# Four edits to the planner's priorities and prices in a Mamba scan kernel: transposes that go ahead of late jobs, gates of six tiles per SiLU, a cheaper GpSimd product, a stricter yield to decays

## The chip, the cores and the metric

The kernel runs on one core of a Trainium2 chip. The core has five engines with an instruction queue each: TensorE (PE in the profile, its weight loads PEld), VectorE (DVE), ScalarE (ACT), GpSimd (POOL) and SyncE (SP), which issues the DMAs. Each queue is worked off in order; semaphores hold an instruction until its inputs are there. The metric is the device time in microseconds. The profile is of one execution.

## The reference

Two residual layers on x of shape (2, 48, 48, 768). Layer 0 is neighbourhood attention (7 x 7 window, 12 heads). Layer 1 is a Mamba block that scans the 2304 tokens of each image forwards and backwards, with 1536 inner channels and 16 states per channel. All is float32.

```python
x = x + _L0_conv_ref(_gn(x), w_qkv, w_out)              # attention
xz = einsum('bld,ed->bel', _gn(x) as tokens, in_proj_w)  # layer 1
out_f = _branch(xz, ...)
out_b = _branch(xz[:, :, ::-1], ..._b)[:, :, ::-1]
x = x + einsum('bdl,cd->blc', out_f + out_b, out_proj_w)

def _branch(xz, ...):
    x, z = (xz[:, :d_in], xz[:, d_in:])
    x = silu(_dwconv(x, conv_w, conv_b))                 # 4 taps
    dt, Bm, Cm = split(einsum('bdl,ed->bel', x, x_proj_w))
    delta = softplus(einsum('brl,dr->bdl', dt, dt_proj_w) + dt_proj_b)
    A = -exp(A_log)
    # per token: h = exp(delta*A)*h + (delta*x)*B ;  y = sum over 16 states of h*C
    y = _selective_scan(x, delta, A, Bm, Cm) + x * Dp
    return y * silu(z)
```

## The kernel before, in words

**Tiles and passes.** Channels lie on the 128 partitions: 12 channel tiles (ND). Tokens are cut into 6 chunks of 384 (CL). A pass is one chunk in one direction of one image; there are 24 passes of 12 tiles, 288 units. Image 0 goes forwards through its chunks, then backwards, then image 1.

**A unit (`scan`, L1179 on)** has four groups of four states. For each group: the B product (L1224) writes delta*x*B into a buffer hb, on DVE or POOL, as the planner chooses for three groups of the four (the first of them, g = 0, is DVE's alone); four decays exp(delta*A) (L1246, ACT) go two by two into the PSUM buffers da, of which there are two; two scans (L1257, DVE), each over two states, work in place in hb; the C product (L1272, POOL) multiplies hb by C; twelve transposes on PE (L1289, `add_up`) add the four states into py, transposed, after three transposes of x*Dp (L1305, `direct`) that open py. Then ACT copies py to yt (L1315). In a forward pass yt goes to memory. In a backward pass PE turns the sum of both directions back (`sums`, L1342), and DVE multiplies by the gate silu(z) (L1352). There are seven hb, one py and one du (a copy of delta*x in PSUM that DVE's B products read).

**Jobs beside the scans.** The in-projection of a chunk (`in_proj`) makes u (x after its four taps and SiLU, both directions) and the gates z, tile by tile: PE products (L382, mm_xin and mm_z), first taps on ACT (L928), three more per direction on DVE (L935), z copied by ACT (L955). After every KB = 3 tiles, `finish` runs one SiLU over a uz buffer (two of them) and stores it: a table load, the SiLU, a table load back (L961, L962). A u buffer holds three tiles in two directions, 2304 elements a partition; a z buffer holds three tiles, 1152. Softplus of the deltas (L1161, L1162) has two table loads as well. Then there are the x_proj products (mm_xd), the attention of image 1 (image 0's runs before the first scan) and the out-projections.

**What sets the order.** Nothing is issued as it is written. `Order.add` records each piece of work with its engine, an estimated time in ns, a key (in units: when it is wanted) and the buffers that it reads and writes. `Order.run` then plans: on each engine it looks at the ready works and picks the one with the lowest rank, the pair (start, but no less than 150 ns after the engine comes free; key - early). So among works that can start at once, the key decides, and a job with an old key goes ahead of the scan's own work. Works marked due are the decays, so this has effect on ACT alone: a work with a later key than the oldest unfinished scan work is put back by half of what it would delay the soonest decay beyond DUE ns. Where PE would idle long, filler transposes are put in (L1489). The program is issued in the planned order, so the estimates set the order only; the chip sets the times.

**Gate chunks.** Image 0's chunk 0 makes its gates late, by an `in_proj` without conv that has keys 41 to 47, and so do chunks 0 to 3 of image 1.

Of the kernel before, what the change touches and what calls it, by code (L numbers as in the profile page):

```python
# [16 lines left out]
P = 128  # L17
# [22 lines left out]
CL = 384  # L40
# [3 lines left out]
SG = 4  # L44
# [49 lines left out]
class Order:  # L94
# [3 lines left out]

    SEM = 90.0
    LOOK = 2.5  # L100
    DUE = 300.0
    GAP = 800.0
    TAIL = {"PE": 120.0, "ACT": 50.0, "DVE": 45.0, "POOL": 10.0, "SP": 0.0}

# [141 lines left out]
def tile_kernel(  # L246
# [72 lines left out]
    def sb(tag, shape, n, parts=1):  # L319
        return Buf(f"{tag}_{n}", wk, shape, tag, BUFS.get(tag, 1), parts)  # L320
# [8 lines left out]
    def add(eng, ns, fn, key, r=(), w=(), job=False, size=0, after=None, early=0, alt=None, due=False, opens=None):  # L329

        news = [x[0] if isinstance(x, tuple) else x for x in w]

        def issue():
            for v in news:
                if v.ap is None:
                    v.ap = v.pool.tile(v.shape, F32, tag=v.tag, name=v.name, bufs=v.bufs)
            fn()

        if eng == "PE":

            ns *= 1.04 if key < 0 else 1.05
        return order.add(eng, ns, issue, key, r, w, job, size, after, early, alt, due, opens)
# [4 lines left out]
    def act(n, pointers=0):  # L347
        return 60 + 90 * pointers + n * 0.833

    def dve(n):  # L350
        return 55 + n * 1.042
# [528 lines left out]
    def in_proj(b, i, start, end, conv=True, gate=True, nk=KB, tags=("uz",), banks=("mm",), proj=None):  # L880
# [67 lines left out]
        def z_tile(k, kk, nk, uz, s, key):  # L948
            m = f"{b}_{i}_{k}"
            part = (uz, s * nk + kk)  # L950
            (wz,) = weights(w_inT, [(0, DI + k * P)], f"z{m}", key, after=got)
            pz = ps("mm", f"z_{m}")
            product(pz, cl, [(wz, c, 0) for c in range(NC)], [(xc, c, HALO) for c in range(NC)], key, to=part)
            add(
                "ACT", act(cl), lambda: nc.scalar.copy(uz[:, s, kk, :cl], pz[:, :cl]), key + 0.05,  # L955
                r=[pz], w=[part], job=True,
            )

        def finish(k0, nk, uz, dsts, key):
            def silu():  # L960
                nc.scalar.activation(uz[:, :, :, :cl], uz[:, :, :, :cl], AF.Silu)  # L961
                nc.scalar.preload_act_table_set("natural_log_exp_and_others")  # L962

            add("ACT", 2600 + act(len(dsts) * nk * cl), silu, key, r=[uz], w=[uz], job=True)
            for s, dst in enumerate(dsts):
                add(
                    "SP", 400,
                    lambda s=s, dst=dst: nc.sync.dma_start(
                        rows_of(dst, k0, nk, l0, cl), uz[:, s, :, :cl]
                    ),  # L970
                    key + 0.1, r=[(uz, range(s * nk, (s + 1) * nk))],
                    w=[(dst, cols(l0, cl, k0, nk))], job=True, size=nk * P * cl * 4,
                )
# [3 lines left out]
        for x, k0 in enumerate(range(0, ND, nk)):  # L977
            if conv:
                uz = sb(tags[x % len(tags)], [P, 2, nk, CL], f"u{b}_{i}_{k0}", 2 * nk)
                for kk in range(nk):  # L980
                    k = k0 + kk
                    u_tile(k, kk, nk, uz, start + k * step, banks[k % len(banks)])
                finish(k0, nk, uz, dsts[:2], start + (k0 + nk) * step)
                if proj:
                    proj(uz, k0, nk, start + (k0 + nk) * step + 0.05)
            if gate:
                uz = sb(tags[x % len(tags)], [P, 1, nk, CL], f"z{b}_{i}_{k0}", nk)
                for kk in range(nk):
                    z_tile(k0 + kk, kk, nk, uz, 0, start + (k0 + kk) * step)
                finish(k0, nk, uz, dsts[-1:], start + (k0 + nk) * step)  # L990

    def staged(src, l0, cl, n, key, w=None, wsrc=None):

# [185 lines left out]
    def scan(ch, k, x, dlj, duj, vt):  # L1179
# [30 lines left out]
        def group(g):  # L1210
            m = f"{n}_{g}"
            now = at + 0.25 * g
            hb = sb("hb", [P, SG * W], m, SG + 1)
            body = (hb, range(SG))
            kept = lambda o: state[:, k, 2 * SG * g + o : 2 * SG * (g + 1) + o].rearrange(
                "p (j e) -> p j e", e=2
            )
            was = zero if ch["first"] else kept(0) if back else kept(1)

            def first():
                by, on = (dus[:, ju, :], nc.gpsimd) if filled.eng == "POOL" else (du[:, :W], nc.vector)
                on.tensor_mul(  # L1224
                    cells(hb, SG), by.unsqueeze(1).to_broadcast([P, SG, W]), bc[g].ap
                )

            if k == 0 or not ch["first"]:
                add(
                    "ACT", 98, lambda: nc.scalar.copy(bc[g][:, :, ends], was), now - 0.4,  # L1230
                    [(state, k * NSG + g)], [(bc[g], 1)], early=EARLY,
                )
            on = {"DVE": dve(SG * W), "POOL": SG * W * 2.2 + 20}
            main, other = ("DVE", "POOL") if g in (0, 1) else ("POOL", "DVE")
            filled = add(
                main, on[main], first, now - (0.35 if main == "POOL" else 0.1),
                [du, duj, bc[g]], [hb], after=marks.get(marks["n"] - 6),
                alt=(other, on[other]) if g in (1, 2, 3) else None,
            )

            def step(j):
                i = g * SG + j
                da = das[j // 2 % 2]
                add(
                    "ACT", act(cl, 1) + 45,
                    lambda: nc.scalar.activation(  # L1246
                        cells(da, 2)[:, j % 2, h], dl[:, jd, c], AF.Exp, scale=q["A"][:, k, i : i + 1]
                    ),
                    now + 0.06 * j - 0.06, [dlj], [(da, j % 2)], due=True,
                )  # L1250

            def two_steps(j):
                da = das[j // 2 % 2]
                at2 = (slice(None), slice(j * W, (j + 2) * W))
                mark = add(
                    "DVE", (4 * W + 42) / 0.96,
                    lambda: nc.vector.tensor_tensor_scan(  # L1257
                        flip(hb[at2]), flip(da[:, : 2 * W]), flip(hb[at2]), 0.0, ALU.mult, ALU.add
                    ),
                    now + 0.06 * j, [da], [(hb, (j, j + 1, SG))],  # L1260
                )
                marks[marks["n"]] = mark
                marks["n"] += 1

            for j in range(0, SG, 2):
                step(j)
                step(j + 1)
                two_steps(j)

            add(  # L1270
                "POOL", SG * cl * 2.03 + 10,
                lambda: nc.gpsimd.tensor_mul(  # L1272
                    cells(hb, SG)[:, :, h], cells(hb, SG)[:, :, h], bc[NSG + g][:, :, c]
                ),
                now + 0.25, [body, bc[NSG + g]], [body],
            )
            if not ch["final"]:
                add(
                    "ACT", 90,
                    lambda: nc.scalar.copy(  # L1280
                        kept(0)[:, :, 1:2], cells(hb, SG)[:, :, leaves : leaves + 1]
                    ),
                    now + 0.3, [body, (hb, SG)], [(state, k * NSG + g)],
                )

            def add_up():
                for j in range(SG):
                    for t in range(nt):
                        nc.tensor.matmul(  # L1289
                            py[:tp, t * P : (t + 1) * P], cells(hb, SG)[:, j, h][:, tb[t]], ident,  # L1290
                            start=False,
                            stop=g == NSG - 1 and j == SG - 1 and t == nt - 1,
                            is_transpose=True, skip_group_check=True,
                        )

            add(
                "PE", SG * nt * 109 + 60, add_up, now + 0.45, [body, py], [py],
                opens=False if g == NSG - 1 else None,
            )

# [6 lines left out]
                    is_transpose=True, skip_group_check=True,  # L1307
                )

        add("PE", nt * 109 + 60, direct, at + 0.3, [vt], [py], opens=True)  # L1310
        for g in range(NSG):
            group(g)
        yt = sb("yt", [P, CL], n)
        w, y0 = nt * P, l0
        add("ACT", act(w), lambda: nc.scalar.copy(yt[:tp, :w], py[:tp, :w]), at + 1.22, [py], [yt])  # L1315
        here = cols(l0, cl, k)
        if not back:
            add(
# [26 lines left out]
                        skip_group_check=True,  # L1345
                    )

        add("PE", 6 * 109, sums, at + 1.28, [yl, yt, zs], [yb])
        (y, yk) = ch["ys"][k] if ch["ys"] else (zs, None)
        into = lambda: y[:, c] if yk is None else y[:, yk, c]  # L1350
        add(
# [62 lines left out]
        "po": ("mm",), "vw": ("w",) * 3, "ev": ("ev",),  # L1414
    }
    LATE = 4
    HEAD = ("bc4", "bc5", "bc6", "bc7", "bc0", "bc1")
    A0, A1, P1 = (-56, -16), (50, 118), 118
    norms, norms0, stats = [], [], []
# [120 lines left out]
```

## Time and profile before

| what | us |
|---|---|
| median of three runs | 7138.75 (7138.43 to 7145.83) |
| the profiled execution | 7136.52 |
| its span, first to last instruction | 7134.7 |
| first scan / last scan | 1053 / 7100 |
| POOL C products, L1272 x1152 | 3654.8 busy, 3187 ns each |
| ACT decays, L1246 x4608 | 2675.6 busy, 584 ns each |
| PE transposes into py, L1289 x13824 | 1756.0 busy |
| PE filler transposes, L1489 x4550 | 577.8 busy |
| ACT waiting with a decay for a scan | 880.4 |
| POOL waiting with a C product for a scan | 393.3 |

The profile's groups are told by line, engine, operation and tiles, as out<-in, with the number of instructions, busy time and mean duration; then the idle time of the engine just before them and what ended it. A busy PE is not a PE at its peak, since its ends are modelled. Attention of image 0 fills the first 1050 us, with DVE half idle; from there on the scans run, with jobs of other stages beside them.

### The profile page before, as it was taken

The numbers are of one execution on the slowest core, as the hardware profiler recorded it, in microseconds if no ns is written. First come the engines' busy times: TensorE is split into PE (matmuls) and PEld (weight loads), VectorE is DVE, ScalarE is ACT, GpSimd is POOL, SyncE is SP. The second block draws the span as 40 slices with busy tenths as digits, with TensorE's granted clock in tenths as the row PEclk, the third lists the DMA queues.
The fourth block names the chain that finished last, engine by engine and source line by source line (L and its number), as shares of the span: only waits on it lengthen the run. The fifth ranks groups of instructions, "written<-read, shape, count | busy, mean of one in ns | idle before, by whom it ended". The sixth has DMA issues, their size and how long they took to land. (4 is left out here: it accounts for less than half of the span.)

```text
span 7134.7 us, 106084 instructions
## 1 busy us (share of the span) xinstructions
PE 6368.7 (89%) x38270; PEld 4910.8 (69%) x38270; DVE 6076.3 (85%) x6222; ACT 5032.7 (71%) x11020; POOL 5435.1 (76%) x1946
## 2 busy tenths in 40 slices
PE   7999988888899999999889888888888898899888
PEld 5666656666667767777666666666678887777777
DVE  1353548998888998989899999999999999999998
ACT  1332348888887787878888677778877667778775
POOL 0000018889888989988878799899899999999997
PEclk9999989999999999999999999999999999999999
DMA  6565453444456454554443453343466676655553
GB/s 190 172 201 178 130 165 118 140 150 130 153 159 204 137 156 140 166 176 121 127 144 108 134 178 101 106 129 113 133 179 195 173 217 196 182 165 169 158 172 109
DMA packets 1338085, 1101.35 MB, mean 154 GB/s; under 512 B 136712, under 2 KB 1327800, under 8 KB 1337528
## 3 DMA queue, kind: packets, MB, share of 16 engines
q1 hardware_dynamic: 1337560, 1094.57, 51.4%
q8 instruction: 303, 4.96, 0.3%
q14 instruction: 222, 1.82, 0.1%
HBM read 881.41 MB, written 213.57 MB: 153 GB/s over the span
## 5 line engine op out<-in xcount | busy, mean ns | idle before, releaser
L1257 DVE TENSOR_TENSOR_SCAN hb<-da,hb 128x772 f32<-128x772 f32 x2304 | 3925.3, 1746 | 226.7 <-ACT da L1246 197.5
L1272 POOL TENSOR_TENSOR hb<-hb,bc 128x1536 f32<-128x1536 f32 x1152 | 3654.8, 3187 | 472.1 <-DVE hb L1257 393.3
L1246 ACT ACTIVATE da<-dlt,A 128x384 f32<-128x384 f32 x4608 | 2675.6, 584 | 948.9 <-DVE hb L1257 880.4
L1289 PE MATMUL py<-ident,hb 128*128 128x128 f32 x13824 | 1756.0, 281 | 165.5 <-POOL hb L1272 163.7
L1289 PEld LDWEIGHTS py<-ident,hb 128*128 128x128 f32 x13824 | 1601.2, 145 | 346.8 <-POOL hb L1272 245.9
L1224 POOL TENSOR_TENSOR hb<-u,bc 128x1544 f32<-128x1544 f32 x490 | 1568.3, 3202 | 25.6 <-PE py L1289 19.2
L1224 DVE TENSOR_TENSOR hb<-du,bc 128x1544 f32<-128x1544 f32 x662 | 1150.1, 1744 | 75.6 <-ACT du L1201 37.8
L1174 POOL TENSOR_TENSOR u<-dlt,u 128x384 f32<-128x384 f32 x288 | 263.7, 918 | 537.0 <-DMA dtw<-dtT 412.8
L382 PE MATMUL mm_z<-xc,w_z 128*128 128x384 f32 x1728 | 606.7, 492 | 16.1 <-ACT uz_z L955 8.4
L382 PE MATMUL mm_xin<-xc,w_x 128*128 128x390 f32 x1656 | 595.8, 503 | 25.5 <-DVE uz_u L935 15.4
L1489 PE MATMUL py<-ident 128*128 128x128 f32 x4550 | 577.8, 281 | 0.0
L382 PE MATMUL mm_out<-stage_y,w_o 128*128 128x192 f32 x3168 | 542.4, 329 | 17.7 <-DVE xr L1078 11.1
L1489 PEld LDWEIGHTS py<-ident 128*128 128x128 f32 x4550 | 529.5, 145 | 32.9 <-issue 31.4
L382 PEld LDWEIGHTS mm_out<-stage_y,w_o 128*128 128x128 f32 x3168 | 517.6, 191 | 33.3 <-DVE xr L1078 14.7
L382 PEld LDWEIGHTS mm_xin<-xc,w_x 128*128 128x128 f32 x1656 | 313.3, 195 | 250.2 <-issue 37.0
L901 POOL MEMSET xc<- 128x18 f32 x4 | 0.5, 120 | 633.6 <-DVE sm L779 633.6
L382 PEld LDWEIGHTS mm_z<-xc,w_z 128*128 128x128 f32 x1728 | 319.1, 191 | 226.9 <-ACT uz_z L955 16.4
L935 DVE SCALAR_TENSOR_TENSOR uz_u<-mm_xin,conv_w,uz_u 128x384 f32<-128x384 f32 x792 | 427.4, 606 | 42.6 <-ACT uz_u L928 38.3
L382 PE MATMUL mm_qk<-xc_xn,w_qk 128*128 128x384 f32 x1296 | 453.6, 497 | 9.7 <-DVE sm L779 2.8
L1305 PE MATMUL py<-ident,vt 128*128 128x128 f32 x864 | 163.0, 301 | 280.2 <-ACT yt L1315 279.9
L382 PEld LDWEIGHTS mm_qk<-xc_xn,w_qk 128*128 128x128 f32 x1296 | 239.1, 193 | 169.7 <-issue 16.6
L1305 PEld LDWEIGHTS py<-ident,vt 128*128 128x128 f32 x864 | 101.9, 148 | 348.0 <-ACT yt L1315 331.1
(163 smaller groups left out, 6992.0 us busy)
## 6 DMA issues: line engine op xcount, KB each, us to landing
w_o<-in_w_opT SPq DMA_DIRECT2D x264, 384.0 KB
bc<-xdf SPq DMA_DIRECT2D x96, 768.0 KB
bc<-xdb SPq DMA_DIRECT2D x96, 768.0 KB
w_qk<-in_w_qkv SPq DMA_DIRECT2D x144, 384.0 KB
w_x<-in_w_inT SPq DMA_DIRECT2D x144, 384.0 KB
w_z<-in_w_inT SPq DMA_DIRECT2D x144, 384.0 KB
w_ao<-in_w_out SPq DMA_DIRECT2D x72, 384.0 KB
u<-uf SPq DMA_DIRECT2D x48, 576.0 KB
```

Source lines behind the costliest of these rows:

```text
L382: nc.tensor.matmul(acc[:m, o0 : o0 + cl], wb[:, wi, wo : wo + m], xb[:, xi, xo : xo + cl], start=c == 0, stop=c == n - 1,)
L901: nc.gpsimd.memset(xc[:, :, : a - lo], 0.0)
L935: nc.vector.scalar_tensor_tensor(u, px[:, at[j] : at[j] + cl], q["conv_w"][:, k, j : j + 1], u, ALU.mult, ALU.add,)
L1174: lambda j=j: nc.gpsimd.tensor_mul(u[:, j, h], dl[:, j, c], u[:, j, h]), at + 0.06 + 0.25 * j,
L1224: on.tensor_mul(cells(hb, SG), by.unsqueeze(1).to_broadcast([P, SG, W]), bc[g].ap)
L1246: lambda: nc.scalar.activation(cells(da, 2)[:, j % 2, h], dl[:, jd, c], AF.Exp, scale=q["A"][:, k, i : i + 1]),
L1257: lambda: nc.vector.tensor_tensor_scan(flip(hb[at2]), flip(da[:, : 2 * W]), flip(hb[at2]), 0.0, ALU.mult, ALU.add),
L1272: lambda: nc.gpsimd.tensor_mul(cells(hb, SG)[:, :, h], cells(hb, SG)[:, :, h], bc[NSG + g][:, :, c]),
L1289: nc.tensor.matmul(py[:tp, t * P : (t + 1) * P], cells(hb, SG)[:, j, h][:, tb[t]], ident, start=False, stop=g == NSG - 1 and j == SG - 1 a ...
L1305: nc.tensor.matmul(py[:tp, t * P : (t + 1) * P], vt[:, tb[t]], ident, start=t == 0, stop=False, is_transpose=True, skip_group_check=True,)
L1489: nc.tensor.matmul(marks["py"][:, CL : CL + P], ident, ident, start=False, stop=False, is_transpose=True, skip_group_check=True,)
```

## The change

- FIRM = 4.0 units of `early` for the transposes into py (`add_up`, `direct`), for ACT's copy of py and for the sum of both directions (`sums`): each goes on record as if wanted four units sooner, for the choice among ready works only.
- In `in_proj`, gates are gathered over two groups of three tiles: one uz buffer, one SiLU and one store for six tiles.
- The plan's price for a B product on POOL, SG * W = 1544 elements, is 2.03 ns per element and 15 instead of 2.2 and 20. `on` is used for the plan alone.
- DUE is 100 ns instead of 300.

```diff
-    DUE = 300.0
+    DUE = 100.0
...
-            if gate:
-                uz = sb(tags[x % len(tags)], [P, 1, nk, CL], f"z{b}_{i}_{k0}", nk)
-                for kk in range(nk):
-                    z_tile(k0 + kk, kk, nk, uz, 0, start + (k0 + kk) * step)
-                finish(k0, nk, uz, dsts[-1:], start + (k0 + nk) * step)
+
+            if gate and x % 2:
+                uz = sb(tags[x % len(tags)], [P, 1, 2 * nk, CL], f"z{b}_{i}_{k0}", 2 * nk)
+                for kk in range(2 * nk):
+                    z_tile(k0 - nk + kk, kk, 2 * nk, uz, 0, start + (k0 - nk + kk) * step)
+                finish(k0 - nk, 2 * nk, uz, dsts[-1:], start + (k0 + nk) * step)
...
-            on = {"DVE": dve(SG * W), "POOL": SG * W * 2.2 + 20}
+            on = {"DVE": dve(SG * W), "POOL": SG * W * 2.03 + 15}
...
-                "PE", SG * nt * 109 + 60, add_up, now + 0.45, [body, py], [py],
+                "PE", SG * nt * 109 + 60, add_up, now + 0.45, [body, py], [py], early=FIRM,
...
-        add("PE", nt * 109 + 60, direct, at + 0.3, [vt], [py], opens=True)
+        add("PE", nt * 109 + 60, direct, at + 0.3, [vt], [py], early=FIRM, opens=True)
...
-        add("ACT", act(w), lambda: nc.scalar.copy(yt[:tp, :w], py[:tp, :w]), at + 1.22, [py], [yt])
+        add("ACT", act(w), lambda: nc.scalar.copy(yt[:tp, :w], py[:tp, :w]), at + 1.22, [py], [yt], early=FIRM)
...
-        add("PE", 6 * 109, sums, at + 1.28, [yl, yt, zs], [yb])
+        add("PE", 6 * 109, sums, at + 1.28, [yl, yt, zs], [yb], early=FIRM)
...
+    FIRM = 4.0
```

In the built programs the instructions differ in number where the edits touch them: 48 SiLU of 1152 elements become 24 of 2304, the table loads of L961 and L962 fall from 98 to 74 each, 48 gate stores of 576 KB become 24 of 1152 KB, B products are 657 on DVE and 495 on POOL instead of 662 and 490, and filler transposes are 4431 instead of 4550. All else is the same in number and stands in another order.

## The prediction

> **What bounds the kernel now.** Read first was the page: span, busy times, slices. A unit below is one channel tile of one chunk in one direction: 288 units, eight scans each. The diff leaves the first 1050 us alone (TensorE's order is the same up to there), so what counts is the stretch with scans, from 1050 to 7100 us.
>
> ```profile
> span 7134.7 us, 106084 instructions
> PE 6368.7 (89%) x38270; PEld 4910.8 (69%) x38270; DVE 6076.3 (85%) x6222; ACT 5032.7 (71%) x11020; POOL 5435.1 (76%) x1946
> DVE  1353548998888998989899999999999999999998
> ```
>
> DVE fills the last third to nine tenths. The windows say how full:
>
> ```profile
> 2000.00:2200.00 200.00, 180.17 (x868) 128.78 (x867) 148.22 (x114) 153.34 (x298) 149.99 (x55) 0.97 0.69 204
> 2200.00:2400.00 200.00, 181.28 (x1154) 147.87 (x1153) 194.67 (x122) 150.25 (x339) 189.96 (x70) 0.98 0.51 146
> 5200.00:7000.00 1800.00, 1602.62 (x10456) 1408.65 (x10454) 1740.21 (x1197) 1325.41 (x2790) 1690.50 (x607) 0.97 0.63 181
> ```
>
> The third number after the window is DVE, the fifth POOL. Where few jobs run beside the scans DVE is busy 96.7% of the time and POOL 93.9%: there only work taken off DVE helps. One stretch stands out, 2000 to 2200 us: DVE idles 51.8 of 200 us, against 5.3 in the next. From 1100 to 7060 us DVE is busy 5570 of 5960 us. The 390 us left are what an order of work can win, and the waits of DVE in that window name most of them:
>
> ```profile
> DVE hb L1257 <- ACT da L1246: 192.3, 133, 5.8
> DVE hb L1224 <- PE py L1289: 34.6, 6, 28.6
> DVE hb L1224 <- ACT du L1201: 28.5, 30, 3.4
> DVE uz_u L935 <- ACT uz_u L928: 23.5, 24, 2.7
> ```
>
> The columns are total, times and longest. Half of it is scans that wait for decays from ScalarE. The second line is nearly all one wait, and the timeline shows it:
>
> ```profile
> 2145.16 11.78 PE L382 MATMUL mm_z<-xc,w_z 128*128 128x384 f32 x36
> 2158.22 4.10 PE L382 MATMUL mm_xd<-stage_u,xpw 128*80 128x192 f32 x24 [1.28 <-DMA xpw<-in_x_proj_w_b]
> 2162.16 4.04 PE L382 MATMUL mm_z<-xc,w_z 128*128 128x384 f32 x12
> 2166.03 1.47 PE L1289 MATMUL py<-ident,hb 128*128 128x128 f32 x12
> ...
> 2167.61 1.76 DVE L1224 TENSOR_TENSOR hb<-du,bc 128x1544 f32<-128x1544 f32 x1 [28.61 <-PE py L1289]
> ```
>
> TensorE runs late jobs (the gates of chunk 0, x_proj products) ahead of the transposes that read hb. With all seven hb in use, DVE's next B product has nowhere to write and the whole scan stands for 28.6 us.
>
> **The change part by part.**
>
> **Transposes first (FIRM).** No instruction is added; key - 4 units moves the sums' transposes, yt's copy and the last sum ahead of jobs up to four units late. In the changed program's order the twelve gate tiles of chunk 0, which stood between units 45.9 and 47.8, lie between 45.4 and 51.1, one or two between each group of transposes. So the 28.6 us and the 2.9 us just before it (same releaser) go. About 8 us more of that window's 51.8 I count, out of 12.0 us of waits for decays between 2030 and 2170 us: four table blocks stood there within 43 us (2114.6 to 2157.4), and they spread too. Sum -40 us. Bounds: -52 (the whole idle time) and 0 (the pile moves as one). What is late next are the jobs: image 2's attention ends its first tile at unit 87.2 instead of 78.4, and the x product of its first chunk at 143.0 instead of 139.2, with that chunk's scan at 144. Before, the second store of that product was issued at 4148.9 us and the scan began at 4261.0: 112 us of room. 3.8 units at 23.6 us each (units 138 to 143) take 90, which leaves 22. A load of that kind took 4.6 us to be usable (issued at 2142.35, its waiting copy at 2146.96); store, load, three delta products, one 3.76 us softplus block, a 0.92 us product and a 1.74 us fill come to about 17 us if the store lands like the load. I count +5 us, from 0 to +22. A longer wait of TensorE at a transposed tile costs only TensorE: its 578 us of filler transposes and about 660 us of idle time in that window cover it.
>
> **Gates of six tiles.** SyncE stores half as often (24 times 1152 KB for 48 times 576 KB). ScalarE's groups:
>
> ```profile
> L961 ACT ACT_TABLE_LOAD x98 | 125.7, 1283 | 1.6
> L961 ACT ACTIVATE uz_u<-uz_u 128x2304 f32<-128x2304 f32 x44 | 93.7, 2129 | 5.6 <-DVE uz_u L935 5.0
> L961 ACT ACTIVATE uz_z<-uz_z 128x1152 f32<-128x1152 f32 x48 | 55.9, 1165 | 0.5
> ```
>
> 48 gate blocks of 3.76 us (load, SiLU, load) become 24 of 4.84, the length of the u blocks. That takes 48 x 1.283 + 24 x (2 x 1.165 - 2.129) = 66 us off ScalarE, but ScalarE is 71% busy and waits for scans 859 us itself, so this is not time won. What counts is how long DVE runs dry in a block. Two pairs of decays lie ahead of it at most, two scans of 1.70 us, and DVE's other work. Sorting DVE's 254 waits by the block that they overlap or follow within 1.5 us gives 31.4 us for the 48 gate blocks without the 28.6 (0.65 each), 73.3 us for the 44 u blocks (1.67 each), 56.9 for the 96 softplus blocks. So 24 x 1.67 - 31.4 = +9 us: this part loses a little. Bounds: -31 (all hidden) and 24 x 5.85 - 31 = +109, with the longest wait of any u block:
>
> ```profile
> 1652.80 2.12 ACT L961 ACTIVATE uz_u<-uz_u 128x2304 f32<-128x2304 f32 x1 [0.72 <-DVE uz_u L935]
> ...
> 1661.94 3.42 DVE L1257 TENSOR_TENSOR_SCAN hb<-da,hb 128x772 f32<-128x772 f32 x2 [5.85 <-ACT da L1246]
> ```
>
> There six normalisations stood behind the block. I take 1.67, the row of the same shape. A uz buffer is now held for six gate tiles, but the last in-projection of chunks 2 and 3 stands at units 16.0 and 25.6 in the new order, 16.2 and 26.0 in the old, so nothing comes late by that.
>
> **Stricter yield (DUE 100).** It reorders ScalarE alone, the only engine with due work. 86.7 us in 79 of DVE's waits for decays lie outside all table blocks, behind bunches of copies. In the orders, stretches between two decays with 2 us or more of other ScalarE work and no table load, each instruction taken at its mean duration, fall from 131 to 98, by a quarter. So -22 us. Bounds: -87, and +52 if DVE's waits for the copies that now stand back (du 28.5, first taps 23.5) double.
>
> **GpSimd's measured price.** The plan's price of a B product falls from 3417 to 3149 ns:
>
> ```profile
> L1224 POOL TENSOR_TENSOR hb<-u,bc 128x1544 f32<-128x1544 f32 x490 | 1568.3, 3202 | 25.6 <-PE py L1289 19.2 <-ACT bc L1230 4.5 <-issue 1.8
> L1224 DVE TENSOR_TENSOR hb<-du,bc 128x1544 f32<-128x1544 f32 x662 | 1150.1, 1744 | 75.6 <-ACT du L1201 37.8 <-PE py L1289 34.6 <-POOL hb L1272 1.7
> ```
>
> Only five products move: 657 on DVE, 495 on POOL. 5 x 1.744 = -9 us on the engine that binds; 5 x 3.2 = 16 us on POOL, inside its 610 us of idle time. Without that cover it would be +16.
>
> **Sum.** -40 + 5 + 9 - 22 - 9 = -57 us. The profiled execution took 7136.5 us (its span 7134.7 and 1.8 around it), so 7079.5; the median of the three runs shown lies 2.2 us higher: 7082 us.
>
> **The rivals.** *Only DVE's work counts.* Waits that vanish come back elsewhere, since DVE and POOL hold each other (POOL waits 385 us for scans), and only the five products are won: 7139 - 9 = 7130. For it: 1740 of 1800 us busy in the late stretch. Against it: 34.6 us have a releaser that is no part of that balance. The Trainium skill, Perfetto Trace Analysis, section "Identifying the Most-Contended Engine", says to judge VectorE by its share of busy time and to optimise the busiest engine first; by that rule alone this rival would hold, yet its next section sends one to the gaps, and the gap of 28.61 us is there.
>
> *The pile moves.* Held jobs come due together near units 84 or 138 to 145 and stall the scan there for as much as was won at 2139 us: -57 + 40, and 15 more where that chunk's chain fills its 22 us of room, 7122 to 7137. For it: the later units above. Against it: no unit of the new order before the last asks TensorE for 22 us of work or more, while in the old one unit 47 asks 30.
>
> *Long blocks stall the scan (slower).* Each six-tile block costs as much as the worst u block, 5.85 us: -57 + 24 x (5.85 - 1.67) = +43, 7182 us. It decides from 1.67 + 57 / 24 = 4.0 us per block. For it: a gate's and a u's block now stand close together (units 11.75 and 12.0 for chunk 2). Against it: 43 of 44 u blocks cost less, and the 3.76 us ones stood as close.
>
> **How the numbers follow.** Forecast 0.66, only DVE's work 0.12, the pile moves 0.08, long blocks 0.14. A change under 0.2% (14 us) cannot be told from none here. Faster by more: the forecast and three quarters of the moved pile, 0.72. Same: 0.10, most of the first rival (9 us) and of a pile that ends near zero. Slower: 0.18, the long blocks and the rest, where held copies (+52) spoil it. The likeliest case alone spans 7040 to 7110 (yield between -60 and 0, the rest near its value). The range must leave only 0.2 out: low 7035, where the yield wins most of its 87; high 7155, past both middle rivals.
>
> **What would show it.** Right: no DVE wait over 10 us, DVE near 190 us busy in each 200 us from 2000; 74 loads on the SiLU line of 1.28 us; DVE's waits around six-tile gate blocks near 40 us in all; waits for decays under 180 us. Wrong: DVE's idle time in the stretch with scans at 390 us or more, a new long wait at the boundary of unit 144, or gate blocks with 4 us of DVE idle each.

## The result and the profile after

The changed kernel takes 7054.33 us (median of 4 runs, 7052.67 to 7056.32), the kernel before 7142.29 (4 runs, 7138.43 to 7147.27): a ratio of 0.988, 95% interval 0.9868 to 0.9891. The gain is 88 us where 57 were forecast (7082 us, between 7035 and 7155). Lines of the kernel before move by one behind the gates: L1246 is L1247 now, L1257 is L1258, L1289 is L1290.

The page of the changed kernel, its span, busy times and DVE's slices:

```profile
span 7054.5 us, 105645 instructions
PE 6334.5 (90%) x38151; PEld 4844.6 (69%) x38151; DVE 6061.2 (86%) x6217; ACT 4970.2 (70%) x10948; POOL 5447.5 (77%) x1951
DVE  2354449999999999998898999999999999999998
```

DVE's busy time fell by 15 us only, the span by 80. From the first scan to the last, 6047 us became 5961: DVE's busy time went from 5649 to 5633 and its idle time, every gap counted, from 398 to 328. So some 70 us of the gain are waits that are gone. The windows of the changed kernel that answer to those of before (DVE is the third number, POOL the fifth):

```profile
2000.00:2200.00 200.00, 178.37 (x977) 133.29 (x977) 181.81 (x122) 165.33 (x340) 170.51 (x62) 0.98 0.68 198
2200.00:2400.00 200.00, 185.30 (x1186) 149.96 (x1185) 195.69 (x122) 151.18 (x334) 193.46 (x71) 0.97 0.60 175
5200.00:6900.00 1700.00, 1516.96 (x9903) 1322.61 (x9901) 1641.58 (x1134) 1242.46 (x2631) 1626.90 (x582) 0.97 0.63 182
```

From 2000 to 2200 us DVE is busy 181.8 us instead of 148.2; in the late stretch it is at 96.6%, as before. DVE's waits while the scans run (total, times, longest):

```profile
DVE hb L1258 <- ACT da L1247: 155.1, 116, 6.3
DVE uz_u L935 <- ACT uz_u L928: 36.5, 35, 3.9
...
DVE hb L1225 <- ACT du L1202: 16.3, 22, 1.7
...
DVE hb L1225 <- PE py L1290: 9.3, 7, 2.7
```

Waits for decays fell by 37 us, those for TensorE's transposes by 25 and those for du by 12; waits for first taps rose by 13. In the kernel before, TensorE's last transposes ahead of the long wait, and the jobs that began behind them:

```profile
2132.20 1.47 PE L1289 MATMUL py<-ident,hb 128*128 128x128 f32 x12
2133.51 5.97 PE L382 MATMUL mm_z<-xc,w_z 128*128 128x384 f32 x18
```

The timeline of TensorE in the changed kernel, where the late jobs run:

```profile
2073.06 4.04 PE L382 MATMUL mm_z<-xc,w_z 128*128 128x384 f32 x12
2076.94 1.47 PE L1290 MATMUL py<-ident,hb 128*128 128x128 f32 x12
2078.25 4.06 PE L382 MATMUL mm_xd<-stage_u,xpw 128*80 128x192 f32 x24
2082.15 4.04 PE L382 MATMUL mm_z<-xc,w_z 128*128 128x384 f32 x12
2086.02 2.78 PE L1290 MATMUL py<-ident,hb 128*128 128x128 f32 x24
2088.64 2.10 PE L382 MATMUL mm_z<-xc,w_z 128*128 128x384 f32 x6
```

In these lines jobs stand for no more than 8 us between two groups of transposes, where they stood for 33 us before (2133.5 to 2166.0); a little later they stand for 11 us once (2122.9 to 2134.3). The wait of 28.61 us has no successor. The groups of the SiLU line and the B products:

```profile
L961 ACT ACT_TABLE_LOAD x74 | 94.9, 1283 | 1.3
L961 ACT ACTIVATE uz_z<-uz_z 128x2304 f32<-128x2304 f32 x24 | 51.1, 2130 | 0.3
...
L1225 POOL TENSOR_TENSOR hb<-u,bc 128x1544 f32<-128x1544 f32 x495 | 1584.6, 3203 | 22.6 <-PE py L1290 14.9 <-ACT bc L1231 4.0 <-ACT state L1281 2.9
L1225 DVE TENSOR_TENSOR hb<-du,bc 128x1544 f32<-128x1544 f32 x657 | 1141.4, 1743 | 34.3 <-ACT du L1202 24.8 <-PE py L1290 9.3
```

An instruction of these groups takes what it took before; only number and order differ. By stretches of units (us from a unit's first scan to the next stretch's, with DVE's idle time in it, worked out from the traces):

| units | beside the scans | before | changed |
|---|---|---|---|
| 0 to 48 | in-projections of image 0 | 1127 (141 idle) | 1066 (74) |
| 48 to 72 | x_proj, start of attention | 461 (13) | 461 (23) |
| 72 to 132 | attention of image 1 | 1312 (118) | 1302 (113) |
| 132 to 156 | its end, first in-projections of image 1 | 559 (28) | 581 (37) |
| 156 to 192 | in-projections of image 1 | 761 (38) | 736 (21) |
| 192 to 288 | out-projections, late gates | 1828 (59) | 1815 (59) |

The gain sits mainly where in-projections run, 61 and 25 us; units 132 to 156 take 22 us more.

### The profile page after: what moved, and what is told of

It reads as the page before. It is cut to its first block, busy times and chain, and to the rows that moved or that the text cites. A ratio compares the mean times of both kernels' runs of the same rounds, so it can differ in the third digit from the quotient of the medians.

```text
span 7054.5 us, 105645 instructions
## 1 busy us (share of the span) xinstructions
PE 6334.5 (90%) x38151; PEld 4844.6 (69%) x38151; DVE 6061.2 (86%) x6217; ACT 4970.2 (70%) x10948; POOL 5447.5 (77%) x1951
## 4 chain that ended last, share of the span: by engine, by line
DVE 39%; PE 19%; ACT 14%; POOL 12%; issue 9%; DMA 6%; SPq 1%; DVEq 0%; POOLq 0%; ACTq 0%
DVE hb L1258 25%; POOL hb L1273 8%; DVE hb L1225 7%; ACT da L1247 4%; PE mm_qk L382 4%; DVE uz_u L935 4%; POOL hb L1225 3%; PE py L1290 2%; PE mm_ao L382 2%; PE mm_v L382 2%; PE mm_xin L382 2%; ACT uz_u L928 1%; PE da L825 1%; ACT pr L785 1%; ACT L1163 1%
## 5 line engine op out<-in xcount | busy, mean ns | idle before, releaser
L1258 DVE TENSOR_TENSOR_SCAN hb<-da,hb 128x772 f32<-128x772 f32 x2304 | 3924.9, 1746 | 187.3 <-ACT da L1247 155.1
L1247 ACT ACTIVATE da<-dlt,A 128x384 f32<-128x384 f32 x4608 | 2677.2, 584 | 915.2 <-DVE hb L1258 845.8
L1290 PE MATMUL py<-ident,hb 128*128 128x128 f32 x13824 | 1754.3, 279 | 264.3 <-POOL hb L1273 255.2
L1290 PEld LDWEIGHTS py<-ident,hb 128*128 128x128 f32 x13824 | 1570.9, 143 | 523.5 <-POOL hb L1273 413.6
L1225 POOL TENSOR_TENSOR hb<-u,bc 128x1544 f32<-128x1544 f32 x495 | 1584.6, 3203 | 22.6 <-PE py L1290 14.9
L1225 DVE TENSOR_TENSOR hb<-du,bc 128x1544 f32<-128x1544 f32 x657 | 1141.4, 1743 | 34.3 <-ACT du L1202 24.8
L382 PE MATMUL mm_out<-stage_y,w_o 128*128 128x192 f32 x3168 | 560.7, 332 | 18.1 <-ACT dlt L1157 6.4
L1491 PE MATMUL py<-ident 128*128 128x128 f32 x4431 | 550.4, 277 | 0.0
L1491 PEld LDWEIGHTS py<-ident 128*128 128x128 f32 x4431 | 503.3, 143 | 28.9 <-issue 26.0
L785 ACT ACTIVATE pr<-pr,sm 128x308 f32<-128x308 f32 x432 | 234.5, 544 | 127.5 <-DVE sm L779 127.2
```

What stands on the lines that cost most here:

```text
L382: nc.tensor.matmul(acc[:m, o0 : o0 + cl], wb[:, wi, wo : wo + m], xb[:, xi, xo : xo + cl], start=c == 0, stop=c == n - 1,)
L785: nc.scalar.activation(pr[j].ap, pr[j].ap, AF.Exp, bias=sm[:, j : j + 1], scale=-1.0, accum_out=sm[:, 2 + j : 3 + j],)
L1225: on.tensor_mul(cells(hb, SG), by.unsqueeze(1).to_broadcast([P, SG, W]), bc[g].ap)
L1247: lambda: nc.scalar.activation(cells(da, 2)[:, j % 2, h], dl[:, jd, c], AF.Exp, scale=q["A"][:, k, i : i + 1]),
L1258: lambda: nc.vector.tensor_tensor_scan(flip(hb[at2]), flip(da[:, : 2 * W]), flip(hb[at2]), 0.0, ALU.mult, ALU.add),
L1290: nc.tensor.matmul(py[:tp, t * P : (t + 1) * P], cells(hb, SG)[:, j, h][:, tb[t]], ident, start=False, stop=g == NSG - 1 and j == SG - 1 a ...
```

## The experiments

First each part alone, then the whole change without each part. Every one of these kernels has its own order, since the plan is made anew.

**FIRM alone.**

```diff
+    FIRM = 4.0
-..., add_up, now + 0.45, [body, py], [py],
+..., add_up, now + 0.45, [body, py], [py], early=FIRM,
...
```

> FIRM alone on the kernel before. Its order spreads the twelve gate tiles of chunk 0 over units 45.9 to 51.2 (45.9 to 47.8 before) and puts 669 B products on DVE instead of 662. Theory of the prediction (the pile-up on TensorE is worth 40 us and nothing else hangs on FIRM): -40 for the pile, 7 x 1.74 = +12 for the products, about 7114 us against 7142, no DVE wait over 10 us. Rival (FIRM matters at every unit, because hb, py and du come free sooner all along): below 7090 us, with less idle time of DVE in most blocks of units, not only in units 42 to 47. Rival (any new order scatters by some tens of us): DVE's idle time changes by more than 5 us in many blocks, in both directions.

7153.7 us against 7142.1, ratio 1.0015 (1.0006 to 1.0024): slightly slower. The pile-up is gone (units 36 to 48 take 272 us instead of 300, their idle time 34 instead of 65), and DVE's longest wait is 10.2 us. But 60 to 72 take 11 us more, 96 to 108 25 more, 132 to 144 10 more. DVE's idle time over all scans is 405 us, 398 before. Both the first theory and the second fall. The third fits: of the 24 blocks of 12 units, 11 change their idle time by more than 5 us, four down and seven up. The window of units 0 to 48 in three kernels, the kernel before, FIRM alone and gates alone, first DVE (third number):

```profile
1053.40:2180.70 1127.30, 992.41 (x5084) 721.37 (x5083) 985.84 (x830) 914.12 (x1726) 960.47 (x341) 0.96 0.48 146
```

```profile
1052.40:2161.00 1108.60, 973.89 (x5013) 714.03 (x5013) 990.04 (x833) 900.68 (x1711) 954.52 (x340) 0.95 0.47 140
```

```profile
1058.60:2134.70 1076.10, 968.18 (x4938) 695.90 (x4937) 990.16 (x832) 880.13 (x1691) 953.76 (x340) 0.96 0.50 150
```

DVE's work is the same within 5 us; the length of the stretch differs by 51.

**Gates of six tiles alone.**

```diff
-            if gate:
+            if gate and x % 2:
...
-                for kk in range(nk):
+                for kk in range(2 * nk):
```

> Gates of six tiles alone. Theory of the prediction (a 4.84 us block costs DVE 1.67 us, a 3.76 us block 0.65): +9 us, 7135 to 7160, the wait of 28.6 us still there in some form since the transposes are not put first. Rival (ScalarE's 66 us count, because decays are late all along while jobs run): 7090 to 7115 us, and DVE's waits for decays fall by 30 us or more also around u blocks and outside blocks.

7126.3 us, ratio 0.998 (0.997 to 0.9989): faster, so the forecast's sign for this part was wrong. Nor does the long wait stay: its order starts chunk 0's gates at unit 41.6 instead of 45.9 and spreads them to 47.5, and units 36 to 48 take 243 us instead of 300. So gates alone undo the pile-up, without FIRM. Units 0 to 48 gain 51 us (the window above); units 72 to 132 give 26 back, units 192 to 288 another 13.

**Yield alone.**

```diff
-    DUE = 300.0
+    DUE = 100.0
```

> DUE 100 alone. In its order the stretches of 2 us or more of other ScalarE work between two decays without a table load fall from 127 to 106 (94 in the whole change). Theory of the prediction: 86.7 us x 21 / 127 = -14 us, 7125 to 7132, with the long wait on TensorE still there. Rival (held copies come late, du and the first taps): 7142 or above, DVE's waits for du and first taps up by what the waits for decays lose.

7149.6 us, ratio 1.001 (1.0 to 1.002): no gain. Waits for decays are 193.0 us (197.5 before), and the long wait is still there:

```profile
DVE hb L1224 <- PE py L1289: 47.9, 9, 28.3
```

Neither theory's sign holds: waits for du and first taps did not rise either (30 and 26 us while scans run, 29 and 26 before).

**GpSimd's price alone.**

```diff
-            on = {"DVE": dve(SG * W), "POOL": SG * W * 2.2 + 20}
+            on = {"DVE": dve(SG * W), "POOL": SG * W * 2.03 + 15}
```

> The price of a B product on GpSimd alone. In its order 641 B products stand on DVE and 511 on POOL: 21 moved, where the whole change moved 5. Theory of the prediction (in the late stretch DVE's work binds): -21 x 1.744 = -37 us at most, 7105 to 7120, with DVE's idle time as before. Rival (POOL is as near to its limit): POOL's work grows by 67 us, waits of DVE for POOL grow, 7135 to 7150.

7159.4 us, ratio 1.0021 (1.0012 to 1.003): slower. Its busy times and the first of its DVE waits:

```profile
PE 6389.1 (89%) x38302; PEld 4919.5 (69%) x38302; DVE 6044.0 (84%) x6201; ACT 5032.3 (70%) x11020; POOL 5499.1 (77%) x1967
...
DVE hb L1257 <- ACT da L1246: 225.1, 159, 6.5
```

DVE has 32 us less to do, as reckoned, but while scans run it idles 449 us instead of 398. Of these 51 us, 28 are waits for decays. Its waits for POOL grew from 10 to 21 us, so the rival's mechanism is there, but it is the smaller part.

Together the four alone give +20 us, the whole change -88. Two readings were left: parts that need each other, or parts that add and a scatter from order to order.

**The whole change without one part.** The edits are those above, taken back one at a time in the changed kernel:

```diff
-..., add_up, now + 0.45, [body, py], [py], early=FIRM,
+..., add_up, now + 0.45, [body, py], [py],
...
```

> The whole change without FIRM. The four parts alone gave +11.5, -15.8, +7.5 and +17.3 us, together -88, so they do not add. Theory of joint cause (in the stretches with in-projections, units 0 to 48 and 156 to 192, each part alone already gained, gates -68 us, FIRM -20, yield -12, price -14, and gave it back elsewhere): without FIRM that stretch stays short, since six-tile gates alone spread chunk 0's gates over units 41.6 to 47.5; 7070 to 7105 us. Theory of the prediction (FIRM carries the largest part): the pile is back, a wait of 20 us or more, 7095 to 7115. Theory of scatter (each new order is a new draw, and the changed kernel a lucky one): 7120 to 7160.

7066.8 us, ratio 0.9896 (0.9878 to 0.9914): 12.5 us slower than the whole. No long wait returns (longest 7.3 us); units 0 to 48 take 1074 us. FIRM does not carry the gain.

```diff
-            if gate and x % 2:
+            if gate:
```

> The whole change without six-tile gates. Theory of joint cause: gates carry most of the gain between units 0 and 48, so 7095 to 7130 us. Theory of the prediction (gates cost 9 us): 7045. Theory of scatter: 7120 to 7160.

7109.4 us, ratio 0.9954 (0.9937 to 0.9971): 55 us of the 88 go with the gates. Units 0 to 48 take 1097 us, 132 to 156 611. There is no pile-up here (units 42 to 47 idle 14.5 us), and yet units 0 to 48 take 31 us longer than in the changed kernel. DVE's waits for decays in these units, without six-tile gates and in the changed kernel:

```profile
DVE hb L1257 <- ACT da L1246: 64.2, 30, 9.6
```

```profile
DVE hb L1258 <- ACT da L1247: 41.3, 20, 6.3
```

ScalarE is busy 902 us of this stretch without them, 869 with them.

```diff
-            on = {"DVE": dve(SG * W), "POOL": SG * W * 2.03 + 15}
+            on = {"DVE": dve(SG * W), "POOL": SG * W * 2.2 + 20}
```

> The whole change without the new price. Its order puts 671 B products on DVE, where the changed kernel has 657: 14 x 1.74 = 24 us more on DVE. Theory of the prediction (DVE's work binds): 7054 + 24 = 7078. Theory of scatter: 7120 to 7160, with other idle time in many blocks.

7085.9 us, ratio 0.9927 (0.9909 to 0.9945): 32 us slower than the whole, near the 24 reckoned. DVE's idle time is the whole change's (331 us for 328), its busy time 30 us higher (5663 for 5633), 25 of them in B products. (These two are from the profiled execution, which took 7099.6 us, 14 above the median.)

```diff
-    DUE = 100.0
+    DUE = 300.0
```

> The whole change without the stricter yield. Its order has 124 stretches of 2 us or more of other ScalarE work between two decays without a table load, 94 in the changed kernel, and 661 B products on DVE instead of 657. Theory of the prediction: 22 us and 7 us, 7083. Theory of scatter: 7120 to 7160.

7105.4 us, ratio 0.9948 (0.9928 to 0.9967): 51 us slower than the whole, nearly twice the 22 + 7 reckoned. DVE idles 370 us instead of 328, in a profiled execution of 7122.0 us, 17 above the median.

**A new order that means nothing.** To see how far the order alone scatters, 1 ns on the plan's semaphore cost, in the kernel before and in the changed one:

```diff
-    SEM = 90.0
+    SEM = 91.0
```

> The kernel before with the plan's semaphore cost at 91 ns instead of 90: nothing is meant by it, but the order is a new one (666 B products on DVE instead of 662, 4744 filler transposes instead of 4550). A fit of one effect for each part to the ten kernels timed so far gives 7165 us for none of the parts, -9 for FIRM, -44 for gates, -16 for the price, -30 for the yield, and leaves 15 us of scatter; the kernel before lies 23 us below its own fit. Theory of additive parts and scatter: 7165, between 7145 and 7185, so slower than before. Theory of joint cause (the parts need each other, and orders scatter little): 7142, within 8 us.

7154.8 us, ratio 1.0015 (1.0006 to 1.0024): 12 us slower than the kernel before, inside the range of the theory of scatter and outside the other's.

> The changed kernel with the plan's semaphore cost at 91 ns: again a new order and nothing else (656 B products on DVE, 4796 filler transposes instead of 4431). Additive parts and scatter: 7066 by the fit, between 7045 and 7085. Joint cause: 7054, within 8 us. Lucky draw: 7110 or more.

7066.3 us, ratio 0.9888 (0.9875 to 0.9902): 12 us slower than the changed kernel, and 76 faster than the kernel before. So the gain is no lucky draw, and some 12 us mean nothing here: the new order was slower by that much both times. Its stretches 0 to 48 and 156 to 192 take 1069 and 738 us, the changed kernel's 1066 and 736; 72 to 132 takes 1274 for 1302 and 132 to 156 615 for 581. In this pair the scatter sits where attention runs beside the scans; in the pair of the kernel before it is spread, 7 us in units 132 to 156 and 10 in 192 to 288.

**Gates and yield together.**

```diff
+            if gate and x % 2:
...
+    DUE = 100.0
```

> Six-tile gates and the stricter yield, without FIRM and without the price. Additive parts and scatter: 7165 - 44 - 30 = 7091, between 7070 and 7110. Joint cause of three (gates, yield and price each lose 30 to 55 us when one is missing): 7110 or more. 671 B products stand on DVE, so DVE's busy time is near that of no_price, and its idle time should be 350 us or less if gates and yield are what empties the waits.

7099.4 us, ratio 0.9933 (0.992 to 0.9945), where the additive fit said 7091. DVE idles 344 us, waits for decays are down to 123.0 us, the lowest of all, and its busy time is 5664. These two parts together shorten the waits; the price then takes 30 to 38 us of work off DVE (5663 to 5633 with FIRM, 5664 to 5626 without).

**DVE's measured prices too.**

```diff
-                    "DVE", (4 * W + 42) / 0.96,
+                    "DVE", (4 * W + 42) / 0.96 + 50,
...
-            on = {"DVE": dve(SG * W), "POOL": SG * W * 2.03 + 15}
+            on = {"DVE": dve(SG * W) + 80, "POOL": SG * W * 2.03 + 15}
```

> The changed kernel with DVE's prices in the plan set to measured ones as well: a scan 50 ns dearer, a B product on DVE 80 ns dearer. Its order puts 624 B products on DVE and 528 on POOL, 33 moved. If DVE's work binds and POOL's idle time (524 us) takes 33 x 3.2 = 106 us: -33 x 1.74 = -57, about 7000 us. By the fit's price effect (about 1 us for each product moved) 7054 - 33 = 7021, plus or minus 15. Rival (POOL binds as well, and DVE waits for it): 7054 or above, with waits of DVE for POOL over 40 us.

7080.0 us, ratio 0.9908 (0.9894 to 0.9921): 26 us slower than the changed kernel. Both estimates miss; the time lies where the rival put it.

```profile
PE 6381.7 (90%) x38858; PEld 4898.9 (69%) x38858; DVE 6020.4 (85%) x6184; ACT 4972.3 (70%) x10948; POOL 5547.8 (78%) x1984
...
DVE hb L1257 <- ACT da L1246: 171.9, 132, 6.6
```

DVE's busy time fell by 41 us again, its idle time rose by 60 (328 to 388) while scans ran, and its waits for POOL are 25 us, not the 40 of the rival. What grew are waits for ScalarE: du by 26 us, decays by 17, first taps by 14. Why more products on POOL bring them was not settled.

## Why the prediction was right, and where it was not

The kernel before was timed beside each group of runs, and its median was 7142.1 to 7143.2 us each time, so the groups can be compared. Fitting one effect for each part to thirteen kernels (the kernel before, the changed one and all of the above but the last), by least squares on their medians, with FIRM F, gates G, price P, yield D:

| parts | measured | fit |
|---|---|---|
| none; none, 91 ns | 7142.3; 7154.8 | 7163 |
| F / G / P / D | 7153.7 / 7126.3 / 7159.4 / 7149.6 | 7153 / 7121 / 7146 / 7135 |
| G D | 7099.4 | 7093 |
| GPD / FPD / FGD / FGP | 7066.8 / 7109.4 / 7085.9 / 7105.4 | 7077 / 7109 / 7084 / 7095 |
| FGPD; FGPD, 91 ns | 7054.3; 7066.3 | 7067 |

The effects are -10 us for FIRM, -42 for gates, -16 for the price, -28 for the yield, each with a standard error of 8; 13 us of scatter are left (eight degrees of freedom). The kernel before lies 21 us below its fit, so each part alone looked worse than it is. Adding parts and scatter explains all thirteen; that they need each other is not required. It is not excluded either: beside the yield the new price is worth 32 us (without it 7085.9, with it 7054.3) and 33 us (7099.4 and 7066.8), alone it lost 17. A joint term for price and yield, added to the fit, comes out at -31 us with a standard error of 11 and brings the scatter down to 9. It is the largest of the six pairs, so it is a hint and not shown.

- *What bounds the kernel* was read rightly: DVE's busy time in the late stretch hardly moved, and the gain came out of the 390 us of gaps, by 70, and out of products, by 9 us of DVE time.
- *Transposes first, -40.* The gain at that place was sized rightly: units 42 to 47 fell from 51.3 to 10.5 us of idle time, 41 us. Its cause was not: the step put the pile's end down to FIRM, and six-tile gates alone end it as well. FIRM's own effect is -10 plus or minus 8, +11.5 alone and -12.5 as the last part: not told from nothing. With FIRM alone the time won at the pile came back in smaller waits and seven more products elsewhere. The prediction never asked whether another part of the change moved the same jobs.
- *The boundary at unit 144, +5 of 0 to 22.* (The prediction's "image 2" is the one called image 1 here.) Units 144 to 149 idle 16.6 us instead of 3.0, so 13.6: inside its bounds, and more than the 5 taken. The late x product is not seen in it as one wait: no wait of DVE there is longer than 2.3 us, and the larger ones are for decays, first taps, du and the sum of both directions. The whole stretch of units 132 to 156 takes 557 to 615 us in the thirteen fitted kernels, so its 22 us more here are not told from the scatter.
- *Gates of six tiles, +9.* This is the step that failed, in sign: -42. Sorted as in the prediction, the 24 long blocks of the changed kernel carry 24.8 us of DVE's waits, 1.03 each, where 1.67 was taken; over the seven fitted kernels with six-tile gates they carry 17.8 to 44.4 us, 0.74 to 1.85 each, so that price was too high here but not out of reach. The 48 short blocks of the kernel before carry 36.6 when every wait from the first scan on is counted. The larger error is what the reckoning put at nothing: it took the blocks at their own place and left out the other jobs of the same stretch. The waits at u blocks fell too, from 73.3 to 51.2 us (64 to 83 in the six fitted kernels without six-tile gates, 38 to 63 in the seven with them). In units 0 to 48 DVE waits 64 to 80 us for decays without them and 35 to 50 with them, and that stretch takes 1097 to 1129 us against 1066 to 1082: no kernel of either kind lies among the other. The pile-up is only one part of this, as the kernel without six-tile gates has none and still loses 31 us there. ScalarE's busy time fell by 62 us over the whole (5032.7 to 4970.2), which the prediction counted (66) and called no time won. The uz buffers also come free at other times; with gates alone chunk 0's gates start 4 units sooner. Which of the two shortens the waits for decays was not tried apart.
- *Yield, -22.* -28 by the fit, -51 as the last part, +7.5 alone: right in size, within the scatter. Its mechanism is not shown: DVE's waits outside table blocks are 205 us in the kernel without it and 167 in the changed one, but also 205 in the kernel without FIRM, which has the yield, and with the yield alone they are 187 against 177 before.
- *Price, -9.* The order moved five products as counted, and DVE's B products fell by 9 us. (DVE's work fell by 16 us in all. Of the rest, 6 are two small instructions of image 1's normalisation, L463 and L485, which took 3.0 and 3.2 us in this trace of the kernel before and 0.2 each in the changed one.) The fit gives -16; without this part DVE has 30 us more to do and the kernel takes 32 longer. The cover was there: POOL's idle time fell from 622 to 524 us.
- *The rivals.* Only DVE's work: no, its idle time fell by 70 us. The pile moves: no, no wait of its size came back, and the 22 us of units 132 to 156 are within what orders scatter there. Long blocks: no, 1.03 us each where 4.0 would have decided. Most signs that the prediction named came in: no wait of DVE over 10 us (longest 6.3), 74 loads, waits for decays under 180 (155.1). Waits at gate blocks came below the 40 us named, and DVE is not near 190 us in each 200 us from 2000: it is busy 171 to 197 us of them up to 4600, 189 to 198 from there on.
- *The sum.* -57 against -88. By the fit the gates miss by -51 us, FIRM and its boundary by +25 (-10 for -35), yield and price by -6 and -7: -39 in all. The places of the two kernels in the scatter, 21 and 13 us below the fit, give 8 back. That the total was nearer than its two largest parts is luck: their errors have opposite signs.

## What to carry to other kernels

Where a planner makes the order, a part alone is measured with a new order's scatter on top, so a part is judged by several kernels with and without it, and by an order changed by nothing. A stall that one edit is meant to remove may go with another, so of each edit ask which of the stalled jobs it moves. And an edit that takes table loads off an engine that does not bind, in a stretch where they stand between the scans' inputs, can win more than the waits at those loads show.
